# Expert inputs of a top-2 mixture turned by transposing DMAs on two 16-bit halves instead of by TensorE; weights fetched four sets ahead instead of five

## The chip, the cores and the metric

The program runs on one core of one Trainium2 chip (trn2). The metric is the device time of one execution in microseconds (us), lower is better, given as the median of several runs. The engines are TensorE (PE, with its weight loads as PEld), VectorE (DVE), ScalarE (ACT), GpSimd (POOL), and SyncE (SP), which issues nearly all DMAs.

## The reference

The input x is 8 sequences of 1024 tokens with 256 channels, all float32. One layer does two things in turn.

A gated scan: `h` is the RMS-normed layer norm of x; one projection gives q, kv and a; `y[t] = sigmoid(a[t]) * y[t-1] + kv[t]` along the sequence; then `x1 = x + q * y`.

A top-2 mixture of 8 experts on xn = layernorm(x1): a router gives each token two experts with gates; per sequence an expert takes at most 256 tokens (`cap`). Cut to what matters:

```python
expert_inputs  = einsum('GSEC,GSM->EGCM', dispatch, xn)          # gather of rows of xn
layer_w0       = einsum('EGCM,EMH->EGCH', expert_inputs, w0)     # M = 256, H = 1368
layer_w1       = einsum('EGCM,EMH->EGCH', expert_inputs, w1)
hidden         = gelu(layer_w0) * layer_w1
expert_outputs = einsum('EGCH,EHM->EGCM', hidden, wo)
out            = x1 + einsum('EGCM,GSEC->GSM', expert_outputs, combine)
```

For the change it matters that the experts' matrix products contract over M, so a gathered tile of 128 tokens x 256 channels has to be turned, to channels on the partitions, before TensorE can use it.

## The kernel before, in words

Sequences are worked on in four blocks of two. A **unit** is one expert of one block, (n, e), 32 in all. The hidden width is cut into 11 pieces of 128 (the last of 88); a **set** is two pieces of one unit, so a unit has 6 sets, s = 0 to 5 (the last one 88 wide), 192 sets in all. Tokens before the experts go in **token units** of 512, u = 0 to 15, four to a block.

One set is `run_set` (line 1000). It computes both first-layer products with a Strassen-like scheme of seven products. Four of them run into the same PSUM bank z, one after the other on top of what is there, and ScalarE copies z out between them: `z = a11*b11` (seen as z<-xT,w), a copy to SBUF (line 1033, the **first snapshot**), then `z += s2*t2` (z<-tb,sb), a copy (line 1047), `z += s3*t3` (z<-tb,sb), a copy (line 1054, the **third snapshot**), then `z += a22*t4` (z<-tb,w). TensorE may not go on with z before ScalarE has copied it. The other three go to banks pa and pb. Between them lie the second-layer products of an earlier set (line 917, acc), in portions given by the list `shares` (lines 1018 to 1025): for s = 1 it is `[1, 2, 1, 0, 0]`, elsewhere the fourth portion, the one between the third snapshot's source and `z += a22*t4`, is 2 or 3 products.

All engines follow one order written out by hand: each engine's queue holds its instructions in the order in which the program names them. Twice in a set, `pump` (line 1255) emits side work: once in the middle (line 1063, just ahead of `z += a22*t4`) and once at the very end (line 1078). Which side work comes at which pump is planned ahead in `plan` from weights that a step carries (lines 1215 to 1242); the steps of the next block's token units are most of it. A step is a list of parts, one for each engine, and a pump emits all parts of a step at once. One of these steps is ("normed", 1) of a token unit (line 400): `second_norm` scales the second half of the unit's rows into xn on VectorE (line 215), and `keep_xn` (line 321) stores the 512 x 256 float32 rows to HBM (xn_d). The first 110 us, up to the first set, are `front` (line 1086), which orders the same steps by a small model of the engines' times.

The expert inputs come like this. `gather_unit` (line 766) has GpSimd fetch four tiles xg of 128 rows of xn for a unit, in the middle pump of s = 5 two units ahead (for the first unit of a block in the end pump of s = 2 of the unit before). `input_step` (line 777) turns them: for each k of two channel halves, four TensorE transposes into a PSUM bank px (line 786) and one ScalarE copy to xT (line 791). In the steady part it is called by `between` (line 1272), right after the middle pump, so ahead of `z += a22*t4`:

```python
slots = (3, 4) if nxt[1] == 0 or nxt == units[1] else (1, 1)
if nxt in units:
    for k in range(KC):
        if s == slots[k]:
            input_step(*nxt, k)()
```

So for most units both halves are turned in set s = 1 of the unit before. `column_sums` (line 796) makes sums of xT on VectorE in s = 4 and 5. The same `between` also turns finished outputs of the unit before (s = 2 and 5, pt_y, line 983), with a copy by ScalarE (line 881) and a store.

Weights: `load_w` (line 92) and `load_wo` (line 99) fetch a set's weights by SP, `AHEAD` = 5 sets ahead (line 1183, line 1297), with 6 and 7 buffers. SP's queue is in the program's order too.

Of the kernel before, what the change touches and what calls it, by code (L numbers as in the profile page):

```python
# [8 lines left out]
FP = mybir.dt.float32  # L9
I32 = mybir.dt.int32  # L10
BF = mybir.dt.bfloat16
AF = mybir.ActivationFunctionType
ALU = mybir.AluOpType
AX = mybir.AxisListType
# [3 lines left out]
def kernel(  # L18
# [11 lines left out]
    nc = tc.nc  # L30
    P = 128
    B, N, D = x.shape
    NE, _, H = w0.shape
    KC = D // P
    G, S = B, N
    CAP = (int(2.0 * S / NE) + 3) // 4 * 4
    NH = CAP // P
    U = 512
    UT = U // P
    UPG = S // U  # L40
    TPG = S // P
# [4 lines left out]
    GB = 2  # L46
    NB = G // GB
    T = GB * TPG
# [2 lines left out]
    SW = [min(2 * P, H - s * 2 * P) for s in range(NS)]  # L51

    const = ctx.enter_context(tc.tile_pool(name="const", bufs=1))
    wpool = ctx.enter_context(tc.tile_pool(name="weights", bufs=7))
    pa = ctx.enter_context(tc.tile_pool(name="tokens", bufs=1))
    pg = ctx.enter_context(tc.tile_pool(name="gate", bufs=1))
    route = ctx.enter_context(tc.tile_pool(name="route", bufs=2))
    pb = ctx.enter_context(tc.tile_pool(name="experts", bufs=2))
    dram = ctx.enter_context(tc.tile_pool(name="dram", bufs=1, space=bass.MemoryType.DRAM))
# [31 lines left out]

    def load_w(b, e, s):
        lo, w = s * 2 * P, SW[s]
        a = wpool.tile([P, 2, KC, 2 * P], FP, tag="w01", name=f"w01_{b}_{e}_{s}", bufs=6)
        nc.sync.dma_start(a[:, 0, :, :w], w0[e, :, lo : lo + w].rearrange("(k p) h -> p k h", p=P))
        nc.sync.dma_start(a[:, 1, :, :w], w1[e, :, lo : lo + w].rearrange("(k p) h -> p k h", p=P))
        return a
# [10 lines left out]
    with tc.manual_schedule(engines={mybir.EngineType.SP}):  # L108
        xts = {0: load_x(0)}
# [17 lines left out]

    slots = const.tile([P, CAP], BF, tag="slots", name="slots")
    nc.gpsimd.iota(slots, pattern=[[1, CAP]], base=0, channel_multiplier=0,
# [5 lines left out]
    rows = const.tile([P, 2, TPG], FP, tag="rows", name="rows")  # L135
# [35 lines left out]
    def weight_step(k, half):  # L171
# [9 lines left out]
        def scale():  # L181
            nc.scalar.activation(
                wT[:, k, half * 3 * P : (half + 1) * 3 * P], at["pw"][:, : 3 * P],
                AF.Copy, scale=gam[:, k : k + 1],
            )

        return Step(("W", k, half), [("PE", 0.4, turn), ("ACT", 0.58, scale)], banks=1, rank=-1)

    xn_d = [dram.tile([S, D], FP, tag=f"xn{g}", name=f"xn{g}") for g in range(G)]
    y_d = [dram.tile([NE * CAP, D], FP, tag=f"y{g}", name=f"y{g}") for g in range(G)]  # L190
    x1_d = [dram.tile([U, D], FP, tag=f"x1{u}", name=f"x1{u}") for u in range(G * UPG)]
    logits, gates, yrow, tok = {}, {}, {}, {}
# [37 lines left out]
    def unit_steps(u):  # L230

        b, hf = divmod(u, UPG)
        blk, ub = divmod(u, UB)
        t = {}
# [21 lines left out]
        def first_rows(half):  # L256
# [3 lines left out]
            for i in range(half * UT // 2, (half + 1) * UT // 2):  # L260
                nc.scalar.activation(
                    t["h"][:, i, :], xts[u][:, i, :], AF.Identity,
                    bias=t["off"][:, i : i + 1], scale=t["sc"][:, i : i + 1],
# [52 lines left out]
        def second_norm(half):  # L316
            if half == 0:
                t["xn"] = pa.tile([P, UT, D], FP, tag="xn", name=f"xn_{u}", bufs=1)
            scale_rows(t["xn"], xts[u], t["mv"], t["r"][:, 0, :], half)

        def keep_xn():
            xts.pop(u)
            nc.sync.dma_start(
                xn_d[b][hf * U : (hf + 1) * U, :].rearrange("(i p) d -> p i d", p=P), t["xn"]
            )

        def x_channels(k):
            if "xnT" not in t:
# [24 lines left out]
        def step(key, parts, needs, weight, banks=0, then=()):  # L353
            parts = [(p[0], p[1], lambda p=p: p[2](*p[3:])) for p in parts]
            early = 1.5 if key[0] in ("moments", "rows", "hT") else 0.0
            return Step((*key, u), parts, needs, weight, banks, rank=rank - early, then=then)


        w, two = u - 1, range(2)
# [17 lines left out]
        for c in two:  # L377
# [19 lines left out]
                 [("second", 0, u), ("back", 1, u)], 12),  # L397
            step(("normed", 0), [("DVE", 0.82, second_norm, 0)],
                 [("second", 1, u), ("normed", 1, w), ("xnT", 0, w), ("xnT", 1, w)], 10),
            step(("normed", 1), [("DVE", 0.82, second_norm, 1), ("SP", 0.1, keep_xn)],  # L400
                 [("normed", 0, u)], 10),
            Step(None, []),
        ] + [
# [11 lines left out]
    def gate_steps(n, groups):  # L415
# [4 lines left out]
        v = gate_tiles.setdefault(n, {})  # L420
        w = {}
        g0, ng = groups[0], len(groups)
        gs, ts, nt = slice(g0, g0 + ng), slice(g0 * TPG, (g0 + ng) * TPG), ng * TPG
# [9 lines left out]
        def by_tile(tag, shape):  # L433
            a = ten(tag, shape)
            w[tag] = a[:, :, ts] if shape[1] == 2 else a[:, ts]
            return w[tag]
# [21 lines left out]
        def top(r, half):  # L458
            raw = w["raw"]
            if r == 0 and half == 0:  # L460
                by_tile("gt", [P, 2, T])
                by_tile("ms", [P, 2, T])
                by_tile("m", [P, 2, T, NE])
                by_tile("sc", [P, T, NE])
            gt, ms, m, sc = w["gt"], w["ms"], w["m"], w["sc"]
            if half == 0:
                V.tensor_reduce(gt[:, r, :], raw, AX.X, ALU.max)
                tt(sc, raw, over_e(gt[:, r, :]), ALU.is_equal)

                tt(sc, sc, desc.unsqueeze(1).to_broadcast([P, nt, NE]), ALU.mult)  # L470
                return
            V.tensor_reduce(ms[:, r, :], sc, AX.X, ALU.max)
            tt(m[:, r], sc, over_e(ms[:, r, :]), ALU.is_equal)
            if r == 0:
                V.scalar_tensor_tensor(raw, m[:, 0], 0.0, raw, ALU.is_equal, ALU.mult)
# [11 lines left out]
        k = 2 * nt * NE  # L487
# [23 lines left out]

        def places():
            m, cnt = w["m"], w["cnt"]
            pm = by_tile("pm", [P, 2, T, NE])
            pv = w["at"][:, :k].rearrange("p (r t e) -> p r t e", r=2, e=NE)
            tt(pm[:, 0], pv[:, 0], m[:, 0], ALU.mult)
            tt(
                pm[:, 1].rearrange("p (g j) e -> p g j e", g=ng),
                pv[:, 1].rearrange("p (g j) e -> p g j e", g=ng),
                cnt.unsqueeze(2).to_broadcast([P, ng, TPG, NE]),  # L520
                ALU.add,
            )
            tt(pm[:, 1], pm[:, 1], m[:, 1], ALU.mult)
# [33 lines left out]
        def slot_tokens():  # L557

            m, keep = w["m"], w["keep"]
            tn = ten("tn", [P, 2, T, 2, NE], BF)[:, :, ts]  # L560
            kr = ten("kr", [P, 2, 2, T])[:, :, :, ts]
# [15 lines left out]
        def one_hot(gl, part):  # L577
            pos = w["pos"]
            for q in range(part * 4, part * 4 + 4):
                r, j = divmod(q, TPG)  # L580
                t = (gl - g0) * TPG + j
                at = pg.tile([P, CAP], BF, tag="oneh", name=f"oneh_{n}_{gl}_{q}", bufs=16)
                eng = nc.gpsimd if ng < GB and part == 3 else V
# [178 lines left out]
    units = [(n, e) for n in range(NB) for e in range(NE)]  # L762
    sets = [(n, e, s) for n, e in units for s in range(NS)]
    w01, wos, sums, inputs, cols, tbs = {}, {}, {}, {}, {}, {}

    def gather_unit(n, e, groups=range(GB)):
        xs = inputs.setdefault((n, e), [])
        for gl, hh in [(gl, hh) for gl in groups for hh in range(NH)]:
            q = gl * NH + hh
            xg = pb.tile([P, D], FP, tag="xg", name=f"xg_{n}_{e}_{q}", bufs=4)  # L770
            nc.gpsimd.indirect_dma_start(  # L771
                out=xg, out_offset=None, in_=xn_d[n * GB + gl][:, :],
                in_offset=bass.IndirectOffsetOnAxis(ap=tok[n][:, gl, hh, e : e + 1], axis=0),
            )
            xs.append(xg)

    def input_step(n, e, k):

        at = {}

        def turn():
            if (n, e) not in cols:
                cols[n, e] = pb.tile([P, KC, GB, CAP], FP, tag="xT", name=f"xT_{n}_{e}")
            at["pt"] = ps(f"px_{n}_{e}_{k}")
            for q in range(UT):
                nc.tensor.transpose(  # L786
                    at["pt"][:, q * P : (q + 1) * P], inputs[n, e][q][:, k * P : (k + 1) * P], ident
                )

        def keep():  # L790
            nc.scalar.copy(cols[n, e][:, k, :, :].rearrange("p g s -> p (g s)"), at["pt"])

        return Step(("px", k), [("PE", 0.44, turn), ("ACT", 0.59, keep)],
                    [("gather", g) for g in range(GB)], banks=1, rank=-2)

    def column_sums(n, e, half):

# [52 lines left out]
    class Set:  # L850
# [19 lines left out]
        def ten(self, tag, nm, bufs):  # L870
            t = pb.tile([P, 2 * CAP], FP, tag=tag, name=f"{nm}_{self.n}_{self.e}_{self.s}", bufs=bufs)
            return t[: self.hs, self.wide]
# [307 lines left out]
        return [[f for f in a if f.parts == [] or not f.done] for a in lists]  # L1180


    AHEAD = 5
    FRONT = UB + 2

    def load_set(j):
# [25 lines left out]
    with tc.manual_schedule():  # L1212
        last, pending, late = None, [], [[] for _ in range(UB)]
        for n in range(NB):
# [28 lines left out]
            if n == NB - 1:  # L1243
                for i, f in enumerate(last_expert_steps()):
                    at_pump(8 + 2 * i, f)
                for i, (fetch, add) in enumerate(combine_steps(n)):
                    k = PUMPS - 2 * NS + 2 + i * 10 // 16
# [24 lines left out]
            def between():  # L1272
                q = at[0] // 2
                e, s = q // NS, q % NS
                nxt = (n, e + 1) if e + 1 < NE else (n + 1, 0)

                slots = (3, 4) if nxt[1] == 0 or nxt == units[1] else (1, 1)
                if nxt in units:
                    for k in range(KC):
                        if s == slots[k]:  # L1280
                            input_step(*nxt, k)()
                before = (n, e - 1) if e > 0 else (n - 1, NE - 1)
                if s in (2, 5) and before in yts:
                    output_rows(*before, s // 5)
                    if s == 5:
                        yts.pop(before)
# [50 lines left out]
```

## Time and profile before

| | |
|---|---|
| median of 3 runs | 2002.85 us (2002.71 to 2003.93) |
| the profiled execution | 2002.99 us, of which the span from first to last instruction is 2001.2 us |
| busy | PE 98%, DVE 68%, POOL 62%, ACT 34% |
| DMA | 228.87 MB moved, mean 114 GB/s |
| granted TensorE clock | 0.995 of full speed in the mean |
| first set begins | about 109 us after the span's start |

How to read it: the page gives, for one execution, the busy time of each engine over the span, and groups of instructions by line with what ended the idle time before each. Times in the timeline are us from the span's start, then the length, the engine, the line of the kernel, the operation, what it writes and reads, and how many were merged; in brackets the idle time of the engine ahead of it and what ended that. PE rows with one matmul show a length of some 0.38 us, but matmuls overlap: their spacing is what they cost. The time of an execution and its span differ by 1.8 us here.

### The profile page before, as it was taken

To read this page: it belongs to the slowest core of one execution; us is meant where nothing else is said; L and a number is where in the kernel's file an instruction comes from. 1 tells how busy PE (TensorE), PEld (TensorE's weight loads), DVE (VectorE), ACT (ScalarE), POOL (GpSimd) and SP (SyncE) were. 2 spreads that over 40 slices of the span, in tenths; PEclk is the share of its full clock that TensorE was granted. 3 is DMA by queue.
4 is the path that set the end of the run, shared out by engine and by line. 5 is a ranking of instruction groups with operands and counts; after the bars stand their busy time and mean duration, and the time that the engine had idled before them with its cause. 6 is when DMAs were issued, how large, how long until landed. Compare 5 with 4: busy or idle time off the path is not lost.

```text
span 2001.2 us, 27850 instructions
## 1 busy us (share of the span) xinstructions
PE 1958.9 (98%) x9402; PEld 1626.9 (81%) x9402; DVE 1365.2 (68%) x2607; ACT 678.5 (34%) x1284; POOL 1239.4 (62%) x1765
## 2 busy tenths in 40 slices
PE   8999999999999999999999999999999999999998
PEld 4568878878888878878888888888888888888887
DVE  5866576677766676857876766667776666766545
ACT  4233333333333323333333333333333333333331
POOL 4356554656455666656656566666766667777657
PEclk9999999999999999999999999999999999999999
DMA  5322423333223434342534243453433344443453
GB/s 179 96 79 74 140 79 109 109 97 111 83 87 110 127 114 144 91 135 88 148 93 122 81 132 110 125 156 111 127 106 110 94 125 137 116 133 100 140 163 94
DMA packets 224078, 228.87 MB, mean 114 GB/s; under 512 B 32448, under 2 KB 215744, under 8 KB 223936
## 3 DMA queue, kind: packets, MB, share of 16 engines
q1 hardware_dynamic: 211104, 193.51, 32.6%
q0 software_dynamic: 12288, 33.57, 5.6%
q8 instruction: 76, 1.25, 0.3%
q14 instruction: 66, 0.54, 0.1%
q10 hardware_dynamic: 544, 0.01, 0.0%
HBM read 185.61 MB, written 41.42 MB: 113 GB/s over the span
## 4 chain that ended last, share of the span: by engine, by line
PE 91%; DVE 5%; issue 1%; ACT 1%; POOL 1%; DMA 1%; SPq 0%; DVEq 0%; ACTq 0%; POOLq 0%
PE z L865 29%; PE acc L917 24%; PE pb L865 15%; PE pa L865 7%; PE pkv L275 3%; PE pq L275 3%; PE pa L275 2%; PE py L897 2%; PE pl L339 1%; PE px L786 1%; PE pt_y L983 1%; PE pt_h L223 1%; PE pt_x L223 1%; PE po L303 1%; ACT sn L1054 1%
## 5 line engine op out<-in xcount | busy, mean ns | idle before, releaser
L821 POOL TENSOR_TENSOR sb<-w 128x256 f32<-128x256 f32 x188 | 128.5, 683 | 443.3 <-PE pb L865 434.4
L865 PE MATMUL z<-tb,sb 128*128 128x256 f32 (+1 forms) x1408 | 368.9, 381 | 5.5 <-ACT sn L1033 5.5
L1056 DVE TENSOR_TENSOR hid<-sn,pb 128x512 f32<-128x512 f32 x192 | 123.0, 640 | 269.4 <-ACT sn L1054 268.8
L865 PEld LDWEIGHTS z<-tb,sb 128*128 128x128 f32 (+1 forms) x1408 | 263.4, 188 | 48.9 <-issue 5.3
L1033 ACT COPY sn<-z 128x512 f32<-128x512 f32 x192 | 105.4, 549 | 433.2 <-PE z L865 433.2
L917 PE MATMUL acc<-hid,wo 128*128 128x256 f32 x840 | 220.8, 379 | 0.0
L917 PE MATMUL acc<-tw,so 128*128 128x256 f32 x900 | 218.7, 379 | 0.0
L1054 ACT COPY sn<-z 128x512 f32<-128x512 f32 x192 | 105.4, 549 | 279.3 <-PE z L865 279.3
L1047 ACT COPY sn<-z 128x512 f32<-128x512 f32 x192 | 105.4, 549 | 270.4 <-PE z L865 270.3
L1041 DVE TENSOR_TENSOR c<-sn,pa 128x512 f32<-128x512 f32 x192 | 122.0, 635 | 104.2 <-PE pa L865 98.4
L865 PE MATMUL z<-tb,w 128*128 128x256 f32 (+1 forms) x704 | 187.1, 384 | 3.8 <-ACT sn L1054 3.8
L917 PEld LDWEIGHTS acc<-tw,so 128*128 128x128 f32 x900 | 171.0, 190 | 24.2
L865 PE MATMUL pb<-xT,sb 128*128 128x256 f32 (+1 forms) x704 | 184.8, 381 | 3.6 <-DVE hid L1056 3.6
L865 PE MATMUL pa<-xT,w 128*128 128x256 f32 (+1 forms) x704 | 184.9, 381 | 1.5 <-DVE hid L1068 1.3
L865 PE MATMUL z<-xT,w 128*128 128x256 f32 (+1 forms) x704 | 184.9, 382 | 0.0
L865 PE MATMUL pb<-tb,sb 128*128 128x256 f32 (+1 forms) x704 | 184.2, 380 | 0.0
L917 PEld LDWEIGHTS acc<-hid,wo 128*128 128x128 f32 x840 | 159.9, 190 | 23.0
L1068 DVE TENSOR_TENSOR hid<-z,c 128x512 f32<-128x512 f32 x192 | 123.1, 641 | 77.7 <-PE z L865 76.8
L991 DVE TENSOR_TENSOR c<-sn,pb 128x512 f32<-128x512 f32 x192 | 122.6, 639 | 58.3 <-PE pb L865 57.6
L824 POOL TENSOR_TENSOR sb<-w,sb 128x256 f32<-128x256 f32 x188 | 155.3, 826 | 0.0
L771 POOL DMA_INDIRECT xg<-xn,tok x128 | 130.6, 1020 | 36.6 <-issue 32.0
L865 PEld LDWEIGHTS z<-xT,w 128*128 128x128 f32 (+1 forms) x704 | 129.1, 188 | 29.3 <-issue 11.1
(179 smaller groups left out, 3767.4 us busy)
## 6 DMA issues: line engine op xcount, KB each, us to landing
w<-in_L_ffn_w_kernel_dram SPq DMA_DIRECT2D x320, 256.0 KB
wo<-in_L_ffn_wo_kernel_dram SPq DMA_DIRECT2D x160, 256.0 KB
y<-ot SPq DMA_DIRECT2D x62, 256.0 KB
xt<-in_L_attn_x_dram SPq DMA_DIRECT2D x16, 512.0 KB
x<-xt SPq DMA_DIRECT2D x16, 512.0 KB
xn<-xn SPq DMA_DIRECT2D x16, 512.0 KB
xc<-x SPq DMA_DIRECT2D x16, 512.0 KB
out_dram<-xc SPq DMA_DIRECT2D x12, 512.0 KB
```

The lines of the kernel that those rows point to most:

```text
L275: nc.tensor.matmul(pp, lhsT=wT[:, k, c * P : (c + 1) * P], rhs=t["hT"][:, k, :], start=(k == 0), stop=(k == KC - 1),)
L771: nc.gpsimd.indirect_dma_start(out=xg, out_offset=None, in_=xn_d[n * GB + gl][:, :], in_offset=bass.IndirectOffsetOnAxis(ap=tok[n][:, gl, ...
L821: eng.tensor_tensor(s1, a21, a22, ALU.add)
L824: eng.tensor_tensor(s4, a12, s2, ALU.subtract)
L865: nc.tensor.matmul(ps[:hs, i * CAP : (i + 1) * CAP], lhsT=a[:, i * hs : (i + 1) * hs], rhs=b, start=first and i == 0, stop=True, skip_grou ...
L917: nc.tensor.matmul(ys[n, e, i][:, half * CAP : (half + 1) * CAP], lhsT=lhsT, rhs=rhs, start=fresh, stop=True, skip_group_check=True,)
L991: nc.vector.tensor_tensor(st.c12, st.snap1, st.cut(st.pb), ALU.add)
L1033: A.copy(snap0, zz)
L1041: V.tensor_tensor(c11, snap0, st.cut(p_a), ALU.add)
L1054: A.copy(snap2, zz)
L1056: V.tensor_tensor(st.h2[: st.hs, 1, st.wide], snap2, st.cut(p_b), ALU.add)
L1068: V.tensor_tensor(st.h2[: st.hs, 0, st.wide], zz, c11, ALU.mult)
```

## The change

Rows of xn are now kept in HBM as two 16-bit halves: for each row first the 256 low halves of the float32 numbers, then the 256 high ones, the same 1 KB. ScalarE makes this form (`halves`, a copy of 2048 16-bit numbers on each partition) in the step ("normed", 1), ahead of the store. For the first two sequences the plain float32 rows are stored as well (xn_first), from which the very first unit is gathered and turned as before. For the 31 other units `turn_inputs` turns each gathered tile, seen as 128 x 512 16-bit numbers, by one transposing DMA from SP, SBUF to SBUF, into a tile `turned` (one buffer), and two ScalarE copies, `join_halves`, of 1024 16-bit numbers each, put the halves of a channel half together as float32 in xT. The transposes of a unit are called in s = 0 and the two copies in s = 1 and s = 2 (for the first unit of a block: transposes in s = 3, both copies in s = 4; for unit (0, 1): s = 2 and s = 3). To make room in SBUF, weights are fetched 4 sets ahead with one buffer fewer of each kind, and two scratch tiles of the routing (sc and pm) lie in a tile that is free at that time.

```diff
-    wpool = ctx.enter_context(tc.tile_pool(name="weights", bufs=7))
+    wpool = ctx.enter_context(tc.tile_pool(name="weights", bufs=6))
...
-        a = wpool.tile([P, 2, KC, 2 * P], FP, tag="w01", name=f"w01_{b}_{e}_{s}", bufs=6)
+        a = wpool.tile([P, 2, KC, 2 * P], FP, tag="w01", name=f"w01_{b}_{e}_{s}", bufs=5)
...
-    xn_d = [dram.tile([S, D], FP, tag=f"xn{g}", name=f"xn{g}") for g in range(G)]
+    xn_d = [dram.tile([S, 2 * D], U16, tag=f"xn{g}", name=f"xn{g}") for g in range(G)]
+    xn_first = [dram.tile([S, D], FP, tag=f"xf{g}", name=f"xf{g}") for g in range(GB)]
...
+        def halves():
+            xts.pop(u)
+            t["xh"] = pa.tile([P, UT, 2, D], U16, tag="xh", name=f"xh_{u}", bufs=1)
+            nc.scalar.copy(
+                t["xh"], t["xn"].bitcast(U16).rearrange("p i (d h) -> p i h d", h=2)
+            )
+
         def keep_xn():
-            xts.pop(u)
+            rows = slice(hf * U, (hf + 1) * U)
             nc.sync.dma_start(
-                xn_d[b][hf * U : (hf + 1) * U, :].rearrange("(i p) d -> p i d", p=P), t["xn"]
-            )
+                xn_d[b][rows, :].rearrange("(i p) d -> p i d", p=P),
+                t["xh"].rearrange("p i h d -> p i (h d)"),
+            )
+            if b < GB:
+                nc.sync.dma_start(xn_first[b][rows, :].rearrange("(i p) d -> p i d", p=P), t["xn"])
...
-            step(("normed", 1), [("DVE", 0.82, second_norm, 1), ("SP", 0.1, keep_xn)],
+            step(("normed", 1), [("DVE", 0.82, second_norm, 1), ("ACT", 1.7, halves), ("SP", 0.1, keep_xn)],
...
+    def turn_inputs(n, e):
+
+        turned = pb.tile([P, 2 * KC, GB * CAP], U16, tag="turn", name=f"turn_{n}_{e}", bufs=1)
+        for q, xg in enumerate(inputs.pop((n, e))):
+            nc.sync.dma_start_transpose(turned[:, :, q * P : (q + 1) * P], xg.bitcast(U16))
+        inputs[n, e] = turned
+
+    def join_halves(n, e, k):
+
+        if (n, e) not in cols:
+            cols[n, e] = pb.tile([P, KC, GB, CAP], FP, tag="xT", name=f"xT_{n}_{e}")
+        nc.scalar.copy(
+            cols[n, e][:, k].rearrange("p g s -> p (g s)").bitcast(U16)
+            .rearrange("p (s h) -> p h s", h=2),
+            inputs[n, e][:, k::KC, :],
+        )
...
-    AHEAD = 5
+    AHEAD = 4
...
-                slots = (3, 4) if nxt[1] == 0 or nxt == units[1] else (1, 1)
+                turn = 3 if nxt[1] == 0 else 2 if nxt == units[1] else 0
                 if nxt in units:
+                    if s == turn:
+                        turn_inputs(*nxt)
                     for k in range(KC):
-                        if s == slots[k]:
-                            input_step(*nxt, k)()
+                        if s == max(turn + 1, 1 + k):
+                            join_halves(*nxt, k)
```

More of the change, by code (lines that the diff above doesn't have):

```diff
@@ L11 @@
 BF = mybir.dt.bfloat16
+U16 = mybir.dt.uint16
 AF = mybir.ActivationFunctionType
@@ L463, in top @@
                 by_tile("m", [P, 2, T, NE])
-                by_tile("sc", [P, T, NE])
+                w["sc"] = ten("mt", [P, 2 * GB * NE * TPG])[:, : nt * NE].rearrange(
+                    "p (t e) -> p t e", e=NE
+                )
             gt, ms, m, sc = w["gt"], w["ms"], w["m"], w["sc"]
@@ L513, in places @@
             m, cnt = w["m"], w["cnt"]
-            pm = by_tile("pm", [P, 2, T, NE])
+            pm = w["pm"] = v["mt"].rearrange("p (r t e) -> p r t e", r=2, e=NE)[:, :, :nt]
             pv = w["at"][:, :k].rearrange("p (r t e) -> p r t e", r=2, e=NE)
@@ L770, in gather_unit @@
             xg = pb.tile([P, D], FP, tag="xg", name=f"xg_{n}_{e}_{q}", bufs=4)
+            first = (n, e) == (0, 0)
             nc.gpsimd.indirect_dma_start(
-                out=xg, out_offset=None, in_=xn_d[n * GB + gl][:, :],
+                out=xg if first else xg.bitcast(U16), out_offset=None,
+                in_=(xn_first if first else xn_d)[n * GB + gl][:, :],
                 in_offset=bass.IndirectOffsetOnAxis(ap=tok[n][:, gl, hh, e : e + 1], axis=0),
```

## The prediction

> **What bounds the kernel now.** I read the page's busy times first, then the chain, then the groups of the turning lines, then the timeline set by set.
>
> ```profile
> PE 1958.9 (98%) x9402; PEld 1626.9 (81%) x9402; DVE 1365.2 (68%) x2607; ACT 678.5 (34%) x1284; POOL 1239.4 (62%) x1765
> ...
> PE 91%; DVE 5%; issue 1%; ACT 1%; POOL 1%; DMA 1%; SPq 0%; DVEq 0%; ACTq 0%; POOLq 0%
> ```
>
> TensorE is the bound (98% busy, 91% of the chain); ScalarE and the DMA engines have room. So the question is what TensorE loses with the 256 transposes of line 786. In the timeline eight of them in a row are spaced 0.109 us: 248 of them (31 units) would be 27 us at face value. The timeline says otherwise. Set 127 (s = 1, with the transposes), then set 139 (s = 1 too, but a unit whose inputs are turned in s = 3 and 4, so nothing stands there):
>
> ```profile
> 1400.56 1.03 PE L865 MATMUL z<-tb,sb 128*128 128x256 f32 x4
> 1401.42 1.04 PE L786 MATMUL px<-ident,xg 128*128 128x128 f32 x8
> 1401.68 0.58 ACT L1054 COPY sn<-z 128x512 f32<-128x512 f32 x1 [1.30 <-PE z L865]
> 1402.32 0.70 PE L865 MATMUL z<-tb,w 128*128 128x256 f32 x2
> ```
> ```profile
> 1509.20 1.03 PE L865 MATMUL z<-tb,sb 128*128 128x256 f32 x4
> 1510.32 0.58 ACT L1054 COPY sn<-z 128x512 f32<-128x512 f32 x1 [1.30 <-PE z L865]
> 1510.96 0.48 PE L865 MATMUL z<-tb,w 128*128 128x256 f32 x1 [0.73 <-ACT sn L1054]
> ```
>
> From z<-tb,sb to z<-tb,w it is 1.76 us in both. With s = 1 the fourth portion of `shares` is 0, and TensorE must wait for the third snapshot; the transposes fill just that hole.
>
> **What leaving out the transposes gains.** I measured that stretch in all sets, against the same stretch with the same side work and no px. (a) In 17 sets with s = 1 and no other side work in the middle: 0. (b) In ten sets with s = 1 other work fills the hole already, and px often waits for a bank besides (in set 55, 1.78 us for DVE L311): 1.40, 1.40, 0.92, 1.50, 2.41, 1.50, 0.91 and three times 1.50, together 14.5 us. (c) In the four units turned in s = 3 and 4, eight groups of four at 0.436: 3.5 us. Sum 18.0 us, not 27.
>
> **ScalarE's new copies.** Nearest rows are SBUF to SBUF: 128x512 takes 633 ns (L1055), 88x256 416 ns, so 217 ns for 256 elements more: 1024 elements 1.07 us, 2048 elements 1.93 us. [...] I take 1.07 and 1.93. The 62 joins come right after the middle pump, where ScalarE idles: in set 127 from 1402.8 to the first snapshot of the next set about 3.5 us later. L791 (588 ns, two a unit) goes away there. Cost 0 if the data are there; if that cover were gone, up to 1 us each, 62 us.
>
> The `halves` copies are different, because ScalarE works in order and this one waits for VectorE. Where ("normed", 1) is emitted in a middle pump, its 1.93 us lie in the same idle stretch: cost 0 (units 6, 7, 8, 10, 11, 14, 15; unit 13 about 0.3). But three of the eleven units after the front have it in the end pump of a set, ahead of the next set's first snapshot: VectorE does L215 of xn after L991, L931 and L932, so units 5, 9 and 12. Unit 12:
>
> ```profile
> 952.74 0.59 ACT L1033 COPY sn<-z 128x512 f32<-128x512 f32 x1 [2.33 <-PE z L865]
> ...
> 954.27 1.03 PE L865 MATMUL z<-tb,sb 128*128 128x256 f32 x4
> ...
> 955.05 1.12 DVE L215 TENSOR_SCALAR xn<-xt,bmv_f,r_f 128x256 f32<-128x256 f32 x2
> ```
>
> Now ScalarE takes the snapshot at 952.74, long before L215 ends (956.17). With the copy queued ahead of it, the snapshot starts at 956.17 + 1.9 and TensorE's z<-tb,sb 0.71 later (as from 879.30 to 880.01 below): 2.6 us after L215's end, at 958.8 and not 954.27, so 4.5 us lost. Likewise unit 5: 199.59 + 2.6 against 196.77, 5.4; unit 9: 645.42 + 2.6 against 645.44, 2.6. Sum 12.5 us. The trace has this very thing once already, where the softmax's exponential is queued ahead of a snapshot:
>
> ```profile
> 878.59 0.46 DVE L447 TENSOR_TENSOR raw<-logits,red 128x128 f32<-128x128 f32 x1
> 879.08 0.31 ACT L450 ACTIVATE raw<-raw 128x128 f32<-128x128 f32 x1 [5.44 <-DVE raw L447]
> 879.30 0.57 ACT L1033 COPY sn<-z 128x512 f32<-128x512 f32 x1
> ...
> 880.01 2.04 PE L865 MATMUL z<-tb,sb 128*128 128x256 f32 x4 [3.53 <-ACT sn L1033]
> ```
> ```profile
> 878.70:885.60 6.90, 5.59 (x13) 4.53 (x14) 1.72 (x3) 3.28 (x5) 0.20 (x1) 0.51 0.01 2
> ```
>
> The second fence is the stretches view (PE, PEld, DVE, ACT, POOL, granted clock, DMA, GB/s): after 3.53 us without work the clock was 0.51 for 6.9 us. The set took 17.71 us, set 80 with the same work 11.30: 6.4 us for a 3.53 us wait, so 2.9 more. [...] The trace halves earlier: 2.89 us between two matmuls at 122.75 was followed by half clock, 1.78 us of waiting at 681 was not. I take half a loss for unit 9 too: 7.3 us. `halves` costs 12.5 + 7.3 = 19.8 us. Ends: 0 if the copies went elsewhere; 35 if they are twice as long.
>
> **The transposing DMAs.** The trace has none. 124 of 128 KB each. Lower end: packets of 1 KB take 46 ns and of 352 B 21 ns, so 256 B pieces about 17 ns, 32 for each engine: 0.6 us. [...] I take 1.4[...].
>
> What time have they? Unit 29: gathers issued 1763.7 to 1767.7, landing 4.4 us later (median), the first at 1768.1. Its join is due at 1778.1, and may start as late as 1781.7 before the next first snapshot (needed at 1780.86 + 2.59) holds TensorE up. So 4t + 2.7 (the shortest landing in the trace) must stay below 13.6: t below 2.7 us. At 1.4 they are done at 1776.4, at 0.6 by 1775.4: cost 0. [...]
>
> On SP each transpose waits for its gather, and the weights of four sets later queue behind: some 8 us. They are needed by the row sums two sets (18 us) later at the earliest, so one set less of lead is still covered; without that cover it is a few us a unit. The waits of SP before are for stores (L885, 588 us) and for `load_wo`'s buffers (518 us), and none held TensorE.
>
> **The rest.** xn_first: four more 512 KB stores, 1.5 us of all DMA engines each, in a stretch with DMA at 0.33; 0. Gathers move the same 1 KB rows; 0. sc and pm only follow VectorE's own order; 0. In the front the ScalarE copy of unit 3 sits ahead of the two L405 copies on the way to the last routing (they start 0.98 us after L215 ends): about 1 us, and the order made by the front's model shifts: I take 1.5, from -2 to +5.
>
> **Sum** against the profiled execution, 2002.99: -18.0 + 19.8 + 1.5 + 0.3 = +3.6, 2006.6. The median is 2002.85, 0.14 less: 2006.5.
>
> **The rivals.** *The gain wins*: the copies are shorter or the clock doesn't drop (stalls 8 instead of 20 us): 2003 - 18 + 8 + 1 = 1994; for it: 8 of 11 later `halves` are covered; against: the wait on L215 alone costs most. *The whole 27 us count* (1976) would need TensorE to skip the third snapshot; set 139 speaks against it. *The DMA is too slow*, slower: at `join_halves` ScalarE waits for the transposes and the next set's snapshot waits behind it; it decides from t = 2.7 us and costs 27 x 4 us for each us above: t = 3.4 gives 2003 + 4 + 76 = 2083[...]. [...] against: 34% busy DMA engines and the 13.6 us of window. *It does nothing it says* is excluded: px leaves TensorE in any case.
>
> **How the numbers follow.** A measurement of this kernel tells some 0.2% (4 us) from no change. Likeliest case (sums near zero, 1999 to 2018): 0.54, of which 0.19 within 0.2% and 0.35 slower. Gain wins (1984 to 1999): 0.25. Slow DMA: 0.21, of which half below 2090. Faster 0.25, same 0.19, slower 0.56. The range 1986 to 2085 leaves a tenth above and a little below.
>
> **What would show it.** Right: in sets with s = 1 z<-tb,w waits for L1054; a 2048-element ACT copy of some 1.9 us ahead of L1033 with a PE wait of 2.5 to 5.5 us at three places, each followed by a clock near 0.5; transposes done before the joins, so no ACT wait on DMA. Wrong: join copies that wait for DMA in every unit (then slow DMA); copies near 1 us; no half clock; the front more than 5 us later.

## The result, and the profile after

The changed kernel takes 2005.91 us (median of 20 runs, 2002.49 to 2008.53); the kernel before 2002.76 us (20 runs, 1998.68 to 2004.28). The ratio is 1.0019, with a 95% interval of 1.0012 to 1.0026: slower by some 4 us (2 to 5), with 2006.5 forecast. The profiled execution of after took 2007.87 us (span 2006.1, granted clock 0.991), that of before 2002.99. Runs of one kernel lie up to 6 us apart, and the longer ones mostly show the lower granted clock (after: 0.994 in the shortest run, 0.991 in the longest).

First the page of after: the busy line, then the two groups of TensorE that wait for a snapshot (busy us, mean ns | idle us ahead of them, and what ended it):

```profile
PE 1942.5 (97%) x9154; PEld 1602.6 (80%) x9154; DVE 1365.8 (68%) x2607; ACT 748.7 (37%) x1300; POOL 1239.9 (62%) x1765
...
L899 PE MATMUL z<-tb,sb 128*128 128x256 f32 (+1 forms) x1408 | 370.0, 382 | 18.1 <-ACT sn L1067 18.1
...
L899 PE MATMUL z<-tb,w 128*128 128x256 f32 (+1 forms) x704 | 187.9, 386 | 17.9 <-ACT sn L1088 17.9
```

TensorE has 248 instructions and 16.4 us of busy time less. In exchange it waits longer: before, the same two groups waited 5.5 us (first snapshot, then L1033) and 3.8 us (third snapshot, then L1054), now 18.1 and 17.9. The rise of the second number, 14.1 us, is the hole that the transposes used to fill. In set 127, whose timeline rows were shown for before, it reads now:

```profile
1409.70 1.03 PE L899 MATMUL z<-tb,sb 128*128 128x256 f32 x4
...
1410.82 0.58 ACT L1088 COPY sn<-z 128x512 f32<-128x512 f32 x1 [1.30 <-PE z L899]
...
1411.46 1.13 PE L899 MATMUL z<-tb,w 128*128 128x256 f32 x4 [0.73 <-ACT sn L1088]
...
1411.84 1.34 ACT L824 COPY xT<-turn 128x1024 uint16<-128x1024 uint16 x1
```

From z<-tb,sb to z<-tb,w it is 1.76 us, as before with the transposes. The join follows in the idle time of ScalarE.

The rise of the first number, 12.6 us, is nearly all the copy of halves ahead of a first snapshot, at three places. The timeline of set 8, where token unit 5 has it:

```profile
202.00 1.27 DVE L218 TENSOR_SCALAR xn<-xt,bmv_f,r_f 128x256 f32<-128x256 f32 x2
...
203.30 1.90 ACT L327 COPY xh<-xn 128x2048 uint16<-128x2048 uint16 x1 [5.53 <-DVE xn L218]
...
205.11 0.58 ACT L1067 COPY sn<-z 128x512 f32<-128x512 f32 x1
...
205.83 1.62 PE L899 MATMUL z<-tb,sb 128*128 128x256 f32 x3 [5.67 <-ACT sn L1067]
```

ScalarE stands 5.53 us for VectorE's xn, copies for 1.90 us, and only then takes the snapshot; TensorE has waited 5.67 us. The stretches view of after (us, busy us of PE, PEld, DVE, ACT and POOL with their instructions, granted clock, DMA share, GB/s) around the three such places, sets 8, 52 and 81:

```profile
203.00:210.00 7.00, 4.17 (x11) 3.43 (x12) 1.56 (x3) 3.50 (x4) 1.40 (x4) 0.53 0.50 110
650.00:657.00 7.00, 4.62 (x22) 3.78 (x21) 4.45 (x10) 3.50 (x4) 3.79 (x9) 1.00 0.31 88
964.50:968.00 3.50, 3.50 (x11) 2.79 (x11) 0.00 (x0) 0.24 (x1) 0.00 (x0) 0.59 0.90 256
```

With the waits of 5.67 and 4.29 us the clock fell to one half, with that of 2.38 us (set 52) it did not in this profile.

The new operations, in the view by tile (count, shortest/median/longest ns):

```profile
L817 SPq DMA_TRANSPOSE turn<-xg x124: 1188/1216/2467, 124.8 to 1880.6; - x124
L824 ACT COPY xT<-turn x62: 1330/1340/1370, 154.0 to 1898.2; 128x1024 uint16<-128x1024 uint16 x62
L327 ACT COPY xh<-xn x16: 1889/1898/1912, 37.3 to 1347.4; 128x2048 uint16<-128x2048 uint16 x16
```

A transposing DMA holds SP's queue for 1.22 us, the packets of one and of the next of a unit begin 1.31 us apart in the median, and no join of after waits for one.

Set by set (a set counted from its first z<-xT,w to the next set's):

| | before, us | after, us |
|---|---|---|
| first set begins | 109.39 | 116.10 |
| set 8 | 11.22 | 18.99 |
| set 52 | 10.78 | 13.40 |
| set 81 | 9.07 | 15.28 |
| set 102 | 10.78 | 11.19 |
| ten sets with s = 1 and other side work | | 13.8 less together |
| eight sets with four transposes | | 3.5 less together |
| sets 2 and 74 | 30.76 | 28.47 |
| s = 1 without side work, each | 8.78 | 8.78 |

### The profile page after: what moved, and what is told of

Its sections match the earlier page's. It is cut to its first block, busy times and chain, and to the rows that moved or that the text cites. A ratio compares the mean times of both kernels' runs of the same rounds, so it can differ in the third digit from the quotient of the medians.

```text
span 2006.1 us, 27711 instructions
## 1 busy us (share of the span) xinstructions
PE 1942.5 (97%) x9154; PEld 1602.6 (80%) x9154; DVE 1365.8 (68%) x2607; ACT 748.7 (37%) x1300; POOL 1239.9 (62%) x1765
## 4 chain that ended last, share of the span: by engine, by line
PE 89%; DVE 6%; ACT 2%; issue 1%; DMA 1%; POOL 1%; SPq 0%; ACTq 0%; DVEq 0%; POOLq 0%
PE z L899 29%; PE acc L951 23%; PE pb L899 15%; PE pa L899 7%; PE pkv L278 3%; PE pq L278 2%; PE pa L278 2%; PE py L931 2%; PE pt_y L1017 1%; ACT sn L1088 1%; PE pl L352 1%; DMA xt<-in_L_attn_x_dram 1%; PE pt_h L226 1%; PE po L306 1%; PE pt_x L226 1%
## 5 line engine op out<-in xcount | busy, mean ns | idle before, releaser
L899 PE MATMUL z<-tb,sb 128*128 128x256 f32 (+1 forms) x1408 | 370.0, 382 | 18.1 <-ACT sn L1067 18.1
L899 PE MATMUL z<-tb,w 128*128 128x256 f32 (+1 forms) x704 | 187.9, 386 | 17.9 <-ACT sn L1088 17.9
L899 PEld LDWEIGHTS z<-tb,w 128*128 128x128 f32 (+1 forms) x704 | 122.7, 187 | 52.1 <-ACT sn L1088 30.0
```

Of the source, the lines that this page charges most:

```text
L899: nc.tensor.matmul(ps[:hs, i * CAP : (i + 1) * CAP], lhsT=a[:, i * hs : (i + 1) * hs], rhs=b, start=first and i == 0, stop=True, skip_grou ...
```

## The experiments

Theory: leaving out the transposes is worth some 17 us, since in most sets with s = 1 they only filled TensorE's wait for the third snapshot. It is lost again to ScalarE's 2048-element copies, ahead of a first snapshot and in the front. Rivals: the lead of the weights, the transposing DMAs, SP's queue, or chance. Ratios are to the kernel before, whose medians in the three rounds of runs were 2003.63, 2003.54 and 2002.95 us.

**d_no_turn: the gain alone** (the kernel before; plain_rows is two ScalarE copies of gathered rows to xT, unturned).

```diff
                         if s == slots[k]:
-                            input_step(*nxt, k)()
+                            plain_rows(*nxt, k)
```

> The kernel before, with the 248 TensorE transposes of the steady part left out: ScalarE copies the gathered rows unturned into xT, so the experts compute on unturned inputs and the outputs are others. No transposing DMA, no 16-bit halves, weights five sets ahead. Theory (with s = 1 the transposes only fill the wait for the third snapshot, so they cost 18 to 19 us): 2002.8 - 18.5 = 1984, between 1982 and 1986. Rival (they cost their spacing, 248 x 0.109 = 27 us): 1976.

Measured 1986.22 us, ratio 0.9916 (0.99 to 0.9933), just above the range. Without any transposition 17 us are gained, not 27, and the wait for the third snapshot rises to 18.5 us. The sets that got shorter, and by how much, are those of after (set 55 2.31, set 7 1.41, set 151 1.39), and plain s = 1 sets are unchanged (but for set 139, 0.28 us longer). That the hole limits the gain is shown.

**g_halves: the loss alone** (after, turned by TensorE again, from plain rows stored for all sequences).

```diff
-            if b < GB:
+            if True:
                 nc.sync.dma_start(xn_first[b][rows, :]...
...
-                    if s == turn:
-                        turn_inputs(*nxt)
...
+                        if s == slots[k]:
+                            input_step(*nxt, k)()
```

> The changed kernel, but turned by TensorE as before from float32 rows, which are kept for all sequences beside the halves: the 2048-element copies and both stores stay, the transposing DMAs and the 1024-element joins are gone. Theory (all of the loss is the 2048-element copies, in the front and at three ends of sets; transposing DMAs and joins are free): 2002.8 + 17.0 + 6.7 = 2026, between 2023 and 2030. Rival (transposing DMAs, joins and the shorter lead of the weights carry part of the loss): below 2018.

Measured 2023.93 us, ratio 1.011 (1.0093 to 1.0127). Set by set it differs from after by what the transposes cost (sets 7, 13, 25, 73, 151 and 163: 1.40 or 1.41 each), and sets 8, 52 and 81 keep their waits (5.21, 2.38 and 4.30 us). So the loss needs neither transposing DMAs nor joins. One difference matters for the clock: with the same wait of 2.38 us as in after, set 52 takes 15.09 us here and not 13.40. The stretches view of g_halves, after that wait:

```profile
656.90:660.30 3.40, 3.40 (x10) 2.69 (x9) 0.00 (x0) 0.35 (x1) 0.00 (x0) 0.50 0.99 282
```

The clock is one half for 3.4 us, where after had 1.00.

**e1_mid: the copies only in middle pumps** (after).

```diff
                     while steps and done + steps[0].weight / 2 <= share * (k + 1):
+                        if k % 2 == 1 and steps[0].key and steps[0].key[:2] == ("normed", 1):
+                            break
```

> The changed kernel, but the step with the 2048-element copy is only planned at middle pumps, never at the end of a set ahead of the next set's first snapshot. Theory (a copy that waits for VectorE holds up a snapshot queued behind it): the sets 8, 52, 81 and 102, which were 7.8, 2.6, 6.2 and 0.4 us longer than before, go back to their old length; 2005.9 - 17.0 = 1989, between 1986 and 1993; TensorE's wait for the first snapshot falls from 18.1 to about 5.5 us. Rival (ScalarE simply has more work, which costs wherever it is put): 2000 to 2006.

Measured 1995.25 us, ratio 0.9967 (0.9954 to 0.9979). Sets 52 and 81 are back at 10.78 and 9.07 us, the wait for first snapshots fell from 18.1 to 5.7 us. Set 8 only fell to 14.05, 2.8 above before: in its middle pump the copy, a join and the copy of pt_y (L915) now stand in a row on ScalarE, and TensorE waits for a bank. Timeline of e1_mid:

```profile
203.62 1.90 ACT L327 COPY xh<-xn 128x2048 uint16<-128x2048 uint16 x1 [1.61 <-DVE xn L218]
...
205.43 1.33 ACT L824 COPY xT<-turn 128x1024 uint16<-128x1024 uint16 x1
...
206.63 0.58 ACT L915 COPY ot<-pt_y 128x512 f32<-128x512 f32 x1
...
207.26 1.98 PE L278 MATMUL pkv<-hT,wT 128*128 128x512 f32 x4 [2.56 <-ACT ot L915]
```

The cause is shown; the expected size was too large, since in the middle pump I had counted the copy at nothing, and set 8 pays 2.8 us for it there.

**e2_front: the copy as a step of its own** (after).

```diff
-            step(("normed", 1), [("DVE", 0.82, second_norm, 1), ("ACT", 1.7, halves), ("SP", 0.1, keep_xn)],
-                 [("normed", 0, u)], 10),
+            step(("normed", 1), [("DVE", 0.82, second_norm, 1)], [("normed", 0, u)], 10),
+            step(("stored", 0), [("ACT", 1.9, halves), ("SP", 0.1, keep_xn)], [("normed", 1, u)], 0),
```

(The next unit's ("normed", 0) and the gathers then wait for ("stored", 0).)

> The changed kernel, but in the front the 2048-element copies and the stores of xn are a step of their own, which the loads of the next token rows don't wait for; in the steady part the copy stays in the same pump as before. Theory (the front lost 6.7 us because loads of x stood in SP's queue behind a store that waited for ScalarE's copy, and behind the second store): the first set begins at 109 to 111 us and not at 116.2, total 1999 to 2001. Rival (the front lost it by ScalarE's time on the way to the routing): first set still at 115 to 116, total 2005 to 2006.

Measured 1984.2 us, ratio 0.9904 (0.9886 to 0.9922), which neither side had said. The steps of two token units are blended by their place in their lists, so one step more moved the side work of the steady part too. No copy stands ahead of a first snapshot any more (that wait is 2.9 us in all), and set 74, which had waited since before the change, fell from 16.68 to 13.57. The first set began at 113.12 us, later than meant. As a test of the front this run is inconclusive; as a version it is good.

**f1_shares: the hole filled** (after).

```diff
-            shares = [1, 2, 1, 0, 0]
+            shares = [0, 1, 1, 2, 0]
```

> The kernel after, with one list changed: the portions of second-layer products in sets with s = 1 are [0, 1, 1, 2, 0] and no longer [1, 2, 1, 0, 0], so that two products stand between the third snapshot's source and z<-tb,w, where the transposes stood before. Theory (what the transposes gave up in the plain s = 1 sets was only a hole that TensorE spends waiting for the third snapshot): the group z<-tb,w of after waits 17.9 us in 30 waits for that snapshot; these go away, 2006 - 17 = 1989 us (1986 to 1993), and an s = 1 set without other side work takes some 8.1 instead of 8.78 us. Rival (the hole only moves: the first or second snapshot is waited for instead, since the portions ahead of it are smaller now): within 3 us of after, 2003 to 2008.

Measured 1984.75 us, ratio 0.9904 (0.9886 to 0.9922), 21 us less than after where 17 were expected. The group on the page of f1_shares:

```profile
L899 PE MATMUL z<-tb,w 128*128 128x256 f32 (+1 forms) x704 | 187.0, 384 | 1.7 <-ACT sn L1088 1.7
```

The wait for the third snapshot fell from 17.9 to 1.7 us, the plain s = 1 sets from 8.78 to 7.91 us, and no other wait took its place (the first snapshot's is 18.1 still). The hole is what the change had left unused. It is larger than the 16.2 us of waiting that went: the view counts a wait from a matmul's end, 0.38 us after its start, while matmuls follow each other at 0.22 us, so each of the 30 waits is counted some 0.16 us short; by this estimate 5 us more, 21 in all.

**h_ahead4: four sets of lead alone** (the kernel before).

```diff
-    AHEAD = 5
+    AHEAD = 4
```

(and one buffer fewer of each kind)

> The kernel before with one part of the change alone: weights fetched four sets ahead with one buffer fewer of each kind. Theory (four sets of lead, some 40 us, cover a fetch with room to spare): 2003 us, within 2 us of before, and no TensorE wait on a weight's DMA. Rival (part of the changed kernel's loss is weights that come late): 2006 or more, with waits of TensorE or GpSimd on load_w or load_wo in the profile.

Measured 2000.32 us, ratio 0.9993 (0.9983 to 1.0003): no difference clear of noise, and no TensorE wait on a set's weights. The median lies 3 us below before's, more than the 2 expected, but the runs of both kernels fall into the same groups (near 1999, 2001.5 and 2003 to 2004 us), and only how many fall into each differs. The lead shows no cost.

**j_early: joins that wait for the DMAs** (after).

```diff
-                        if s == max(turn + 1, 1 + k):
+                        if s == turn + k:
```

> The kernel after with each join one set earlier, in the very set whose middle pump issues the transposing DMAs (the second join in the next), so that ScalarE has to wait for the DMAs. It prices the rival of a late DMA. Theory (the DMAs were in time only by the set of lead between them and the joins; ScalarE works in order, so a join that waits holds up the next set's first snapshot and with it TensorE): from after's trace, end of the last transposing DMA + join 1.34 + snapshot 0.71 less the begin of the next set's z<-tb,sb, summed over 30 units, is 28 us, the largest in units 11, 21 and 29 (4 to 5 us each); so 2034 us (2025 to 2045 with half clock after the longest). Rival (the wait is hidden as the joins themselves are): 2006 us within 3.

Measured 2064.03 us, ratio 1.0297 (1.0272 to 1.0322). The waits view of j_early (us in all, times, longest):

```profile
ACT xT L824 <- DMA turn<-xg: 138.2, 29, 10.3
...
PE z L899 <- ACT sn L1067: 56.7, 23, 5.7
```

ScalarE waits 138.2 us for the DMAs, and 39 us of it reach TensorE (its wait for first snapshots is 56.7 us and not 18.1); the clock falls from 0.991 to 0.980, by estimate 0.020 x 2071 - 0.009 x 2006 = 23 us more of TensorE's time lost at half speed: together 62 of the 65 us between the two spans. The mechanism held, the size did not: the kernel is 58 us slower than after, above the whole range, and the 28 us were too few by two terms. A join that waits begins 1.3 to 2.9 us after the last transposing DMA's issue ends, where I had counted 0.1, and half clock was allowed for only after the longest waits.

**q_front: the front's stores off SP's queue** (after).

```diff
-            nc.sync.dma_start(
+            queue = nc.scalar if alone[0] else nc.sync
+            queue.dma_start(
                 xn_d[b][rows, :]...
```

(xn_first's store too)

> The kernel after, where only in the front (the first four token units) the stores of keep_xn and xn_first are issued from ScalarE's queue and not from SP's. Theory (part of the front's loss is SP's queue: loads of x for later units stand behind stores that wait for the ScalarE copy of halves): the first set begins 1.5 to 5 us earlier than the 116.15 us of after, total 2000 to 2004 us. Rival (the front loses by the copies on ScalarE themselves and by the clock, the queue costs nothing): first set at 115 us or later, total 2005 to 2008.

Measured 2008.67 us, ratio 1.0027 (1.0015 to 1.0038), the first set at 115.83: no gain, as the rival said. In after, the chain of the front passes over SP: a load of x (53.79, 6.22 us) was issued behind stores that waited for the copy of halves. In q_front that piece is gone and another has its place. The chain of q_front (start, us, what):

```profile
68.24 1.91 ACT xh L327
...
70.17 0.37 ACTq L334
...
70.58 0.53 ACTq L339
...
71.15 1.07 ACT hT L386 x2
```

The copy, and now the issue of two stores, stand ahead of the copies that the next routing needs. One caution: this profile had 20.5 us of half clock ahead of the first set, that of after 13.7, so a gain of one or two us by the queue could be hidden in it.

**r_front: the front without the copies** (after; first block as before the change).

```diff
-            step(("normed", 1), [("DVE", 0.82, second_norm, 1), ("ACT", 1.7, halves), ("SP", 0.1, keep_xn)],
+            step(("normed", 1), [("DVE", 0.82, second_norm, 1), *[("ACT", 1.7, halves)][b < GB :], ("SP", 0.1, keep_xn)],
...
-            first = (n, e) == (0, 0)
+            first = n == 0
```

> The kernel after, where the first two sequences are handled as before the change: no copy of halves and one float32 store for their four token units, and the eight units of the first block turned by TensorE; everything later as in after. Theory (the front's loss is the four ScalarE copies in it, not the lead of the weights and not chance): the first set begins at 109.4 us (108.5 to 111) and not at 116.15; the total gets 6.7 us less for that and 5.9 us more for the transposes of block 0 (sets 3, 4, 7, 13, 19 and 25 in after gained that much): about 2005 us (2002 to 2008), while the stall at set 8 stays. Rival (the front is late for another reason, such as four sets of lead): first set at 113 us or later, total 2009 or more.

Measured 2006.86 us, ratio 1.0025 (1.0018 to 1.0032), the first set at 110.15 us, and the sets of the first block longer by the 5.9 us expected. So without the four copies and their stores the first set comes 5.9 us earlier in these two profiles; the medians say 5 us (2005.91 + 5.9 - 2006.86).

**best2 and best: the two repairs together.** best2 is e2_front with f1_shares' list.

> The kernel after with two edits: the copy of halves and its stores as a step of their own that follows ('normed', 1) at a later pump (e2_front), and the portions [0, 1, 1, 2, 0] for s = 1 (f1_shares). Theory (the two losses are separate: copies ahead of a first snapshot, and the hole before z<-tb,w): the gains add, 2005.9 - 21.7 - 21.2 = 1963 us (1960 to 1969), waits for the first snapshot below 5 us in all and for the third below 3 us. Rival (moved side work fills the same hole already): 1975 or more.

Measured 1958.93 us (1957.59 to 1961.63), ratio 0.978 (0.9764 to 0.9797). The two groups on the page of best2:

```profile
L899 PE MATMUL z<-tb,sb 128*128 128x256 f32 (+1 forms) x1408 | 367.4, 380 | 2.7 <-ACT sn L1067 2.5
...
L899 PE MATMUL z<-tb,w 128*128 128x256 f32 (+1 forms) x704 | 186.6, 384 | 1.7 <-ACT sn L1088 1.7
```

36 us of waiting have become 4.4. The gains add, and 4 us more came than their sum, just below the range; part of it is the clock (set 65, below). This version beats both kernels, that before by 2.2%.

> The same as best2, and the front's stores issued from ScalarE's queue as in q_front. Theory (the front gains nothing by the queue, as q_front showed in after's order of the front): within 3 us of best2. Rival (with the copies split off, SP's queue is what the front waits for): 3 to 6 us faster than best2, the first set at 108 to 110 us.

best measured 1963.35 us, ratio 0.9804 (0.9788 to 0.9821), 4.4 us above best2 and so outside both expectations; its first set began at 113.53 us (best2: 112.69), set 0 took 1.6 us more and set 65 1.7. No gain from ScalarE's queue is seen. In both of these sets the clock record of best has 3.41 us of half clock (from 114.02 and from 776.20 us), which is up to 1.7 us of TensorE's time, and that of best2 has none there; e2_front has the same 3.41 us in its set 65.

## Why the prediction was right

The mechanism was right: the transposes gave 17 us and not 27, and copies of halves ahead of first snapshots took as much again. The total is better than its terms. Worked through with the profiled executions (us):

| term | forecast | measured |
|---|---|---|
| transposes left out | -18.0 | -17.3 |
| sets 2 and 74 | 0 | -2.3 |
| three stalls at first snapshots | 12.5 | 12.3 |
| half clock after them | 7.3 | 4.3 |
| set 102 | 0.3 | 0.4 |
| front | 1.5 | 6.7 |
| the rest, not followed | 0 | 0.8 |
| sum | 3.6 | 4.9 |

- **The gain.** The count by groups held to 0.7 us: 13.8 for 14.5 in the ten sets, 3.5 in the groups of four, 0 in the plain ones. d_no_turn shows it without the rest of the change, f1_shares shows that the hole was there to be filled.
- **The stalls.** 5.4, 2.6 and 4.5 us were forecast at units 5, 9 and 12; 5.67, 2.38 and 4.29 were measured, with a copy of 1.90 us where 1.93 had been worked out from two lengths of L1055 (an activation, c<-c, and no copy). e1_mid and g_halves show the cause.
- **The clock.** In this profile the sum was too large: 2.1 us at set 8 (7.77 - 5.67), 0.2 at set 52 and 1.9 at set 81. But the term varies from profile to profile. In the clock records of before and after the half clock comes in pieces of 3.41 or 6.83 us (the last, at the end of a trace, apart), and within one trace they begin whole multiples of 3.413 us apart (before: 83.39, 93.63, 124.35 and 878.70, that is 3, 9 and 221 multiples; after: 62.83, 90.13, 103.79, 131.09, 202.77, 885.44 and 963.95, that is 8, 4, 8, 21, 200 and 23). In the first 150 us of the other runs stretches of 2 us add up to the same two lengths. The same waits meet these pieces differently. At set 52, 2.38 to 2.39 us of waiting left the clock alone in after, f1_shares, q_front and r_front, and halved it for 3.41 us in g_halves and j_early. At set 81, 4.29 to 4.30 us brought 3.41 us in after, g_halves and r_front, 6.83 in f1_shares, q_front and j_early. At set 52 I had taken half a loss, so 2.5 times the 2.9 us of set 74 in all; after has none there, g_halves and j_early have one piece, so half a loss was a fair figure. (The 2.89 us at 122.75 that I compared with it is from start to start; as idle time, like the others, it is 2.51 us.) That the place of a wait against the 3.413 us steps decides is argued from this, not tested.
- **Sets 2 and 74** did not get shorter by the turning. Set 74 has its wait of 3.53 us in both kernels, with 6.83 us of half clock before and 3.41 in after; in h_ahead4, which turns by TensorE, it has 3.41 us as well. Set 2 has 3.7 us of half clock in both (before until 131.17, after until 137.92), and is 1.3 us shorter by its side work: four products pq<-hT,wT (1.72 us, at 136.21 before) stand ahead of the first set in after (at 114.38), and four transposes pt_x (0.43 us) are in set 2 for them. What the clock does to this set h_ahead4 shows: without half clock there it takes 11.22 us, 1.8 less than before. (All profiles with this wait and four sets of lead show 3.41 us there, the two with five sets, before and d_no_turn, 6.83; whether the lead has a part in it is not shown.)
- **The front** is the term that was mis-sized: 1.5 us forecast, from -2 to +5, and 6.7 measured. "The front more than 5 us later" was one of the prediction's own signs of being wrong, and it came true. I had counted one copy ahead of two others (1 us) and half a microsecond for the order, and no clock. r_front puts 5 to 6 us on the four copies and their stores. They reach the last routing along more than one way (SP's loads behind stores that wait, the copies for the next routing behind them on ScalarE), and taking away one way, as q_front did, showed no gain. The clock is the second part. From the end of the last routing to the first set, in after and in g_halves, which has the same front:

```profile
103.40:116.10 12.70, 11.86 (x38) 6.41 (x35) 8.62 (x22) 2.55 (x4) 5.68 (x8) 0.73 0.21 62
```
```profile
101.40:111.80 10.40, 9.16 (x38) 4.87 (x36) 8.95 (x22) 2.62 (x4) 5.71 (x8) 1.00 0.25 76
```

  With the same 38 matmuls after needs 2.3 us more, at a clock of 0.73. Over the whole front, five profiles of the same front read: no half clock, first set at 111.7 us (g_halves); 10.2 us of half clock, 114.4 and 114.8 (j_early, e1_mid); 13.7 us, 116.1 (after); 17.1 us, 115.8 (f1_shares). With 10.2 us too, but without the copies, r_front begins at 110.2 (pq ahead of the first set as in after, at 108.44). So at like clock the copies and stores cost some 4 to 5 us. In the rest of the 6.7 are the 1.3 us of products that before has in set 2, and the clock (before had 6.8 us of half clock in its front); these two are not told apart here. What lets the clock fall in one profile of the front and not in another stays open.
- **The joins** took 1.34 us, a quarter more than the 1.07 worked out, and cost nothing, as forecast: the cover was 3.5 us, and the plain s = 1 sets are as long as before.
- **The transposing DMAs.** Forecast 1.4 us each, measured 1.22 us at issue and 1.31 from one to the next. The 0.6 us worked out from the packets of before misses both. The 1.4 us came close, but was my own estimate: the trace of before, which has no transposing DMA, did not show it, nor anything slower for the rival. (The DMA engines were busy 0.39 of the time before, by the stretches view, not 34%; it changes nothing.) j_early shows that the rival of a late DMA had its mechanism right: with one set less of lead the kernel takes 58 us more.
- **Lead of the weights, SP's queue in the steady part.** Nothing to be seen, as forecast (h_ahead4 for the lead; no set of after outside the groups of the table got longer by more than 0.5 us).

So the front cost 5.2 us more than said, and the clock and two other sets 5.3 us less; that these cancelled is luck: much of both sides is where the half clock fell in the two executions that were profiled, and 1.3 us of both is the work that moved from set 2 to the front.

## What to carry to other kernels

Before counting the matmuls that a change removes, look at what the engine does in that place without them: work in a wait is worth nothing until something else is put there (27 us of transposes gave 17, and f1_shares 21 us more). A copy added to an engine that works in order costs less by its length than by how long it waits for its input, and by what is queued behind (1.90 us of copying held TensorE for 5.67 us at set 8, and the two 1.34 us joins of a unit cost nothing); ask at each place whether that is on the bounding engine's path. Moved side work, too, goes to where another plan puts it, so a repair is judged by the whole kernel's time. A term of a few us for the clock varies from profile to profile (none to 17.1 us of half clock in five profiles of one front): take it from several, not from one.

## What the runs showed of the hardware

- SBUF to SBUF on ScalarE, activations of 256 and 512 elements (0.416 and 0.633 us) put 1024 elements at 1.07 us and 2048 at 1.93. The copy of 2048 16-bit numbers, which reads interleaved and writes in runs of 256, took 1.90 us and lies on that line; the copy of 1024, which writes interleaved, took 1.34 and lies 0.27 above it. That the interleaved writing is the cause was not tested.
- A transposing DMA of 128 x 512 16-bit numbers moves its 128 KB in 512 packets of 256 bytes, 18 ns each in the median; 16 DMA engines would need 0.6 us for them, but the DMAs follow each other at 1.31 us in the median, with 1.22 us of issue each. So by these numbers the queue's issue, not the packets, sets the pace.
- The half clock came in pieces of 3.41 or 6.83 us, in before and after on a grid of 3.413 us. A wait of 2.38 us (set 52) drew none or one piece of 3.41, 4.29 us (set 81) drew 3.41 or 6.83, 3.53 us (set 74) 6.83 in before and d_no_turn and 3.41 in after, g_halves and six more, and waits of 5.2 to 5.7 us (set 8) 6.83 in all six profiles.
